# One more GpSimd drain behind an output scatter, in a masked attention layer on one Trainium2 core

## The chip, the cores and the metric

The kernel runs on one core of a Trainium2 chip. Its engines work side by side, each from its own instruction queue: TensorE (PE; its weight loads are shown as PEld), VectorE (DVE), ScalarE (ACT), GpSimd (POOL) and SyncE (SP). Transfers are issued from the queues of SP, ACT and POOL and run on 16 DMA engines. The metric is device time in microseconds for one execution; lower is better. The kernel before takes 637.19 us (median of three runs, 636.75 to 637.22).

## What is computed

One graph attention layer with a norm ahead of it, over 2708 nodes of 1024 features, all in float32:

```python
h = jnp.maximum(_layernorm(x, axis=-1), 0.0)
q = h @ W_q.T + b_q
k = h @ W_k.T + b_k
v = h @ W_v.T + b_v
z = (q @ k.T) / sqrt(1024)
spare_z = z * adj
spare_z = jnp.where(spare_z == 0.0, -10000.0, spare_z)
out = jax.nn.softmax(spare_z, axis=1) @ v
return x + jax.nn.relu(out)
```

The adjacency is sparse: each entry is one with a chance of 0.0014771, about four neighbours for a node.

## The kernel before

The kernel does not form the 2708 x 2708 scores. It folds the two weights of query and key into one matrix `M`, finds the neighbours of each node in `adj`, sorts the nodes by their number of neighbours, and handles 128 sorted nodes at a time (a tile). For a tile it gathers the normed rows of the neighbours one slot at a time, forms the scores and the weighted sum `u` of those rows on VectorE, and multiplies `u` by the value weights on TensorE.

TensorE's work is a list of 20 units (`units`, L1194): ten pairs of tiles for the queries, then ten pairs for the outputs (`o_pairs`, L1192), and one last tile alone. The tiles of the outputs go in the order 6, 5, 4, 3, 2, 0, 20, 7, 17, 13, 18, 12, 19, 11, 15, 10, 14, 1, 16, 9, and tile 8 is the one alone. A pair is multiplied in seven products of blocks (Strassen's scheme in Winograd's form); `multiply` (L1044) issues them, and calls `after(i)` at seven points of each pair, i from 0 to 6. `after` (L1243) interleaves everything else: the attention of later tiles, loads, and the sending of results.

The pair before the last is number `len(units) - 2`, tiles 14 and 1. Its step 2 comes when the second of its products has been copied out.

Results go out like this. ScalarE writes a finished tile `y`; `due` (L1130, L1134) notes at which step it may be sent. `add_due` (L1166) then issues from GpSimd an accumulating gather that adds the rows of `x` in the sorted order to `y` (`add_x`, L1106), and `send` (L1173) issues behind it the scatter of an earlier `y` to its rows of the output (`scatter`, L807). So gathers and scatters alternate in GpSimd's queue, and a scatter belongs to a tile two behind. Every scatter is appended to `outs` (L805). For the last pair and the tile alone, `ends` (L1138) and the code from L1373 gather `x` ahead, and VectorE adds it. The four buffers of the tag "q" hold `y`, so a gather into one waits for the scatter that read it. The tile alone is scattered in two halves (`scatter_half`, L1365).

The order on VectorE is the one written in the code; from L1256 on, the order in GpSimd's queue is made by the tile framework's planner, and `issue_after(ins)` adds a bound, that what it holds is not issued before `ins`.

At the end, `flag` is read by every engine (L1388); it is zero here, and the branch of L1389 skips the general path. When the tile context of L1562 closes, a program end is written: SyncE waits for all outstanding semaphores, every engine drains and the engines meet at a barrier. The program's opening stands at L1555.

Of the kernel before, what the change touches and what calls it, by code (L numbers as in the profile page):

```python
# [65 lines left out]
def tile_preln_masked_attention(  # L66
# [12 lines left out]
    nc = tc.nc  # L79
# [675 lines left out]
    def banks_for(row):  # L755

        return_ = []
        for h in range(NH):
            return_.append(psum.tile([P, NB], FT, tag="acc", name=f"ps{h}"))
            nc.scalar.copy(return_[h], row[:, h * NB:(h + 1) * NB])  # L760
        return return_
# [43 lines left out]
    outs = []  # L805
# [238 lines left out]
    def multiply(n, results, after):  # L1044


        X, Z = banks_of.pop(n)
        ops = ops_of.pop(n)[0]
        Y, p5 = opened_of.pop(n)
        after(0)  # L1050
        after(1)
        products.append(add_block(Y, ops["s2"], T[:, 1]))
        u2 = small("u2")
        nc.scalar.copy(u2, Y)
        after(2)
        add_block(X, ops["a12"], M[:, 1, 0])
        results[0](X)
        after(3)
        products.append(add_block(Z, ops["s4"], M[:, 1, 1]))
        results[2](Z, u2)  # L1060
        after(4)
        products.append(add_block(Y, ops["s3"], T[:, 2]))
        results[1](Y, p5)
        after(5)
        between(n)
        add_block(Y, ops["a22"], T[:, 3])
        results[3](Y)
        after(6)
# [125 lines left out]
    units = [("q",) + p for p in q_pairs] + [("o",) + p for p in o_pairs]  # L1194
# [34 lines left out]
    for n, unit in enumerate(units):  # L1229
# [13 lines left out]
        def after(i):  # L1243
# [81 lines left out]
                single["rows"], = load_rows(("o", alone))  # L1325
            if nxt is None and i == 3:
                single["banks"] = banks_for(bp_sb)
            if n == last_q - 1 and i == 4:

                nc.sync.dma_start(bp_sb, bv.to_broadcast([P, D]))  # L1330
# [235 lines left out]
```

## Time and profile before

| | |
|---|---|
| median of three runs | 637.19 us |
| span of the profiled execution, first to last instruction | 635.2 us |
| PE busy | 624.2 us, 98% |
| DVE busy | 523.9 us, 82% |
| POOL busy | 367.3 us, 58% |
| ACT busy | 285.9 us, 45% |
| granted TensorE clock, mean | 0.996 |

The profiled execution is one of its own. The profile gives its span and no time for what lies before the first instruction and behind the last; the median of the runs is 1.99 us over the span. A row of the page's second part is a strip of 40 slices of the span, each digit the busy share in tenths. In a row of the timeline stand start, duration, engine, line, operation, output and input, and in brackets the idle time before it with what ended it. Names such as POOLq and SPq are an engine's queue (its sequencer): drains, semaphores, branches and DMA issues of SP and ACT stand there, and count as no busy time. A row for one line gives the least, median and largest duration in ns, then the first and last start in us. A row of waits gives the total in us, the number and the longest.

### The profile page before, as it was taken

The numbers are of one execution on the slowest core, as the hardware profiler recorded it, in microseconds if no ns is written. First come the engines' busy times: TensorE is split into PE (matmuls) and PEld (weight loads), VectorE is DVE, ScalarE is ACT, GpSimd is POOL, SyncE is SP. The second block draws the span as 40 slices with busy tenths as digits, with TensorE's granted clock in tenths as the row PEclk, the third lists the DMA queues.
The fourth block names the chain that finished last, engine by engine and source line by source line (L and its number), as shares of the span: only waits on it lengthen the run. The fifth ranks groups of instructions, "written<-read, shape, count | busy, mean of one in ns | idle before, by whom it ended". The sixth has DMA issues, their size and how long they took to land.

```text
span 635.2 us, 6138 instructions
## 1 busy us (share of the span) xinstructions
PE 624.2 (98%) x1627; PEld 316.4 (50%) x1627; DVE 523.9 (82%) x1020; ACT 285.9 (45%) x423; POOL 367.3 (58%) x397
## 2 busy tenths in 40 slices
PE   9999999999999999999999999999999999999993
PEld 5777766444444544444444444444444444444441
DVE  5999888998896755997889999999899999898231
ACT  3538985749667553424341244343343342432200
POOL 2639960885877277564742644586678868622421
PEclk9999999999999999999999999999999999999998
DMA  8999997598796539996599997999999989993851
GB/s 340 407 369 310 342 356 288 203 325 310 261 360 237 182 118 323 342 351 220 188 295 365 307 399 227 322 346 294 386 354 289 336 276 284 278 269 80 242 189 37
DMA packets 62497, 181.16 MB, mean 285 GB/s; under 512 B 10055, under 2 KB 17047, under 8 KB 61688
## 3 DMA queue, kind: packets, MB, share of 16 engines
q0 software_dynamic: 27088, 86.02, 42.6%
q1 hardware_dynamic: 29434, 73.63, 33.2%
q10 hardware_dynamic: 5934, 21.06, 8.5%
q8 instruction: 15, 0.25, 0.1%
q14 instruction: 26, 0.21, 0.1%
HBM read 148.27 MB, written 42.31 MB: 300 GB/s over the span
## 4 chain that ended last, share of the span: by engine, by line
PE 98%; POOL 0%; DVE 0%; POOLq 0%; issue 0%
PE ps L1010 45%; PE psy L1010 32%; PE ps_y L476 6%; PE ps_z L476 4%; PE ps_x L476 4%; PE pt L415 4%; PE ps_y L511 1%; PE ps_h L1222 0%; PE ps_v L594 0%; DVE y_alone L1382 0%; POOL out_dram L1366 0%; POOLq L1388 0%; POOL hsum L121 0%; PE ps_all L680 0%; PE ps_in L678 0%
## 5 line engine op out<-in xcount | busy, mean ns | idle before, releaser
L610 POOL DMA_INDIRECT g<-h_dram,tab x94 | 119.6, 1272 | 62.1 <-ACT u L912 19.1
L1010 PE MATMUL ps<-M,a 128*128 128x512 f32 x320 | 144.0, 593 | 0.0
L1010 PE MATMUL psy<-wlow,s 128*128 128x512 f32 x320 | 143.9, 593 | 0.0
L863 DVE SCALAR_TENSOR_TENSOR junk<-g,pq 128x1024 uint8<-128x1024 f32 x93 | 113.7, 1223 | 12.8 <-DMA g<-h_dram,tab 8.9
L1010 PE MATMUL ps<-M,s 128*128 128x512 f32 x240 | 107.9, 593 | 0.0
L1010 PEld LDWEIGHTS ps<-M,a 128*128 128x128 f32 x320 | 59.9, 190 | 70.7 <-issue 70.0
L1010 PEld LDWEIGHTS psy<-wlow,s 128*128 128x128 f32 x320 | 59.8, 190 | 70.0 <-issue 69.1
L923 DVE SCALAR_TENSOR_TENSOR u<-g,coef,u 128x1024 f32<-128x1024 f32 x69 | 88.4, 1282 | 6.9 <-ACT u L912 5.8
L389 DVE FIND_INDEX8 at<-ones,adj 128x8 uint32<-128x685 f32 (+1 forms) x88 | 74.5, 864 | 0.0
L1010 PEld LDWEIGHTS ps<-M,s 128*128 128x128 f32 x240 | 45.6, 190 | 57.1 <-issue 55.9
L1010 PE MATMUL psy<-wlow,a 128*128 128x512 f32 x160 | 71.9, 593 | 0.0
L368 ACT ACTIVATE sized<-adj 128x2708 uint8<-128x2708 f32 (+1 forms) x22 | 54.3, 2467 | 7.3 <-DMA adj<-in_adj_dram 6.0
L298 POOL TENSOR_TENSOR hsum<-hsum,x 128x256 f32<-128x256 f32 (+1 forms) x56 | 38.6, 726 | 26.2 <-DVE wlow L444 21.6
L1109 POOL DMA_INDIRECT y<-in_x_dram,tab x19 | 32.7, 1723 | 30.5 <-ACT y L1126 15.7
L1010 PEld LDWEIGHTS psy<-wlow,a 128*128 128x128 f32 x160 | 30.5, 190 | 38.2 <-issue 37.5
L1010 PE MATMUL ps<-wlow,s 128*128 128x512 f32 x80 | 36.0, 592 | 0.0
L912 ACT ACTIVATE u<-g,coef 128x1024 f32<-128x1024 f32 x18 | 20.7, 1148 | 29.9 <-DVE coef L911 29.8
L808 POOL DMA_INDIRECT out_dram<-y,tab x21 | 25.3, 1206 | 15.2 <-DVE flag L1357 7.1
L626 POOL DMA_INDIRECT tab_dram<-tab,pos_i x22 | 21.9, 993 | 18.8 <-DVE pos_i L689 13.3
L276 ACT ACTIVATE x<-x,r 128x1024 f32<-128x1024 f32 (+1 forms) x22 | 25.9, 1233 | 7.2 <-POOL r L266 7.2
L944 ACT COPY v<-u 128x1024 f32<-128x1024 f32 x13 | 13.6, 1046 | 32.5 <-DVE u L923 28.2
L476 PE MATMUL ps_y<-wlow 128*128 128x512 f32 x64 | 27.6, 593 | 0.0
(252 smaller groups left out, 851.7 us busy)
## 6 DMA issues: line engine op xcount, KB each, us to landing
adj<-in_adj_dram SPq DMA_DIRECT2D x21, 1354.0 KB, 10.4
x<-in_x_dram SPq DMA_DIRECT2D x21, 512.0 KB, 11.0
h_dram<-x ACTq DMA_DIRECT2D x21, 512.0 KB, 7.3
u_dram<-v ACTq DMA_DIRECT2D x13, 512.0 KB, 6.6
or<-u_dram SPq DMA_DIRECT2D x52, 128.0 KB, 6.4
q_late<-q SPq DMA_DIRECT2D x12, 512.0 KB, 7.1
pq<-q_late POOLq DMA_DIRECT2D x12, 512.0 KB, 8.0
M<-in_wv_dram SPq DMA_DIRECT2D x4, 1024.0 KB, 10.4
```

The source lines that it names most:

```text
L276: nc.scalar.activation(xs[i][:n], xs[i][:n], AF.Relu, bias=r[:n, 4, i:i + 1], scale=r[:n, 3, i:i + 1])
L298: small.append(nc.gpsimd.tensor_add(hsum[:n, cols], hsum[:n, cols], xt[:n, cols]))
L368: nc.scalar.activation(sized[:n], a[:n, :, :PW], AF.Abs, accum_out=total[:n, t:t + 1])
L389: nc.vector.max_index(at[:n, k - first_k, g, :], ones[:n, 0:8], a[:n, g, :])
L415: nc.tensor.transpose(pt[:, c, :], xt[:, k * P:(k + 1) * P], ident)
L476: mm = nc.tensor.matmul(bank, a_tile(o + H * a[0], a[1], i), b(o), start=first and o == 0, stop=(o == H - 1), skip_group_check=True)
L610: return nc.gpsimd.indirect_dma_start(out=dst, out_offset=None, in_=src, in_offset=off, bounds_check=N - 1, oob_is_err=False)
L808: to = nc.gpsimd.indirect_dma_start(out=out, out_offset=bass.IndirectOffsetOnAxis(ap=ptab.bitcast(U32)[:n, t, SLOTS:SLOTS + 1], axis=0), i ...
L863: chained(lambda: nc.vector.scalar_tensor_tensor(junk, g_of[t][s], 1.0, tq[t], op0=ALU.mult, op1=ALU.mult, accum_out=zall[:, t, s:s + 1]))
L923: chained(lambda: nc.vector.scalar_tensor_tensor(u, g_of[t][s], coef[:, s:s + 1], u, op0=ALU.mult, op1=ALU.add))
L1010: mm = nc.tensor.matmul(bank, a[:, c, :], b[:, c, :], start=False, stop=(c == 3), skip_group_check=True)
L1109: return nc.gpsimd.indirect_dma_start(out=y[:n], out_offset=None, in_=x, in_offset=off, compute_op=ALU.add)
```

## The change

Three lines in `after`. When the pair before the last is at step 2, one drain is issued on GpSimd, not before the scatter that was appended last to `outs`. No other line is touched; later lines move down by three.

```diff
@@ -1325,6 +1325,9 @@
                 single["rows"], = load_rows(("o", alone))
             if nxt is None and i == 3:
                 single["banks"] = banks_for(bp_sb)
+            if (n, i) == (len(units) - 2, 2):
+                with tc.issue_after(outs[-1].ins):
+                    nc.gpsimd.drain()
             if n == last_q - 1 and i == 4:
 
                 nc.sync.dma_start(bp_sb, bv.to_broadcast([P, D]))
```

## The prediction

> **What bounds the kernel now.** I read the page first, for the share of each engine and the chain that ended last.
>
> ```profile
> span 635.2 us, 6138 instructions
> PE   9999999999999999999999999999999999999993
> q0 software_dynamic: 27088, 86.02, 42.6%
> PE 98%; POOL 0%; DVE 0%; POOLq 0%; issue 0%
> ```
>
> TensorE sets the pace: the chain is 98% matmul, and no slice but the last shows it idle. A change on GpSimd can matter in two ways only. It makes TensorE wait, or it alters what lies behind the last matmul. So I read the end next: the chain of waits in its last microseconds, then every instruction that stands at line 1562, which is the close of the program (its common barrier).
>
> ```profile
> 615.00 10.42 PE ps L1010 x24
> 625.42 0.02 issue
> 625.45 0.70 DVE y_alone L1382
> 626.15 0.03 issue
> 626.18 0.50 POOLq L1388
> 626.68 0.69 POOL out_dram L1366
> ...
> L1562 SPq EVENT_SEMAPHORE  x14: 17/28/28, 629.7 to 635.2; - x14
> L1562 POOLq EVENT_SEMAPHORE  x4: 17/17/17, 634.4 to 635.1; - x4
> L1562 POOLq DRAIN  x3: 46/109/7122, 627.2 to 634.9; - x3
> L1562 SPq DRAIN  x3: 7/7/13, 630.4 to 634.6; - x3
> L1562 ACTq DRAIN  x2: 8/8/8, 616.5 to 634.6; - x2
> L1562 PEldq DRAIN  x2: 8/8/8, 625.6 to 634.7; - x2
> L1562 DVEq DRAIN  x2: 10/14/17, 629.2 to 634.7; - x2
> ...
> SPq L1562 <- DMA out_dram<-y_alone,half_i: 10.3, 1, 10.3
> SPq L1562 <- PEq L1562: 4.6, 2, 4.1
> ```
>
> The last matmul ends at 625.4, and 9.8 us follow. The chain stops at the last scatter (626.68 + 0.69 = 627.37), since a drain is not counted as work; the rows of line 1562 show what is behind it. They give duration as least/median/most, and the starts of the first and last instruction. ScalarE, TensorE and VectorE come to the barrier at 616.5, 625.6 and 629.2. SyncE first waits for the last scatter to land (its first semaphore row starts at 629.7), goes through the other semaphores and drains at 630.4. GpSimd's first drain starts at 627.2, lasts 7122 ns and so ends at 627.24 + 7.12 = 634.36. Only then do GpSimd's semaphores run, from 634.4. SyncE sits 4.1 us in one wait of this barrier, though the name beside it is that of TensorE's queue, which had arrived at 625.6; GpSimd was the one missing. **So the last 3.9 us before 634.4 belong to GpSimd's drain alone.** SyncE's own arrival is its first drain at 630.42 plus the next about 0.07 later, 630.49, and 634.36 - 630.49 = 3.87.
>
> Then I asked what such a drain costs. The other drains of GpSimd are the two short ones of that row (46 and 109 ns) and one at the opening:
>
> ```profile
> L1555 POOLq DRAIN  x1: 184/184/184, 0.4 to 0.4; - x1
> ```
>
> These three have no transfer of GpSimd between them and the drain or the start before. The long one has all of them: the 27088 packets of the software queue.
>
> **The change, part by part.** It adds one drain on GpSimd and an order (not before the scatter that was issued last); it removes nothing and moves no line. Where it stands:
>
> ```profile
> 571.15 1.57 POOL L1109 DMA_INDIRECT y<-in_x_dram,tab  x1 [9.03 <-ACT y L1133]
> 573.03 1.00 POOL L808 DMA_INDIRECT out_dram<-y,tab  x1 [0.30 <-issue]
> 586.05 1.70 POOL L1109 DMA_INDIRECT y<-in_x_dram,tab  x1 [12.03 <-ACT y L1126]
> 588.06 1.05 POOL L808 DMA_INDIRECT out_dram<-y,tab  x1 [0.31 <-issue]
> 594.34 0.97 POOL L612 DMA_INDIRECT y<-in_x_dram,tab  x1 [5.24 <-DMA out_dram<-y,tab]
> ```
>
> In the pair before the last (tiles 14 and 1), the scatter issued last at step 2 is that of 573.03. GpSimd is then idle from 574.03 to 586.05, waiting 12.03 us for ScalarE's result for tile 14. The drain falls into this hole.
>
> *Cost in the hole.* No row shows a drain in mid-run. From below it is 0.05 us (the 46 ns row). From above it is the whole 7.12 us, and if it first waits for the scatter's landing (median 5.8 us from issue, in the row below, so 578.8), it ends at 585.9. VectorE is busy there 11.45 of 11.80 us, and one scatter's descriptors have taken from 952 to 1884 ns; were the drain stretched by that 1.98, 14.1 us from 574.03 end at 588.1. I take 6.5 us: the last drain runs 634.36 - 627.37 = 6.99 us behind the last scatter, and 25072 of 27088 packets lie before the hole, 93%. It ends near 580.5, under cover of the wait for tile 14.
>
> ```profile
> 574.10:585.90 11.80, 11.80 (x29) 5.18 (x28) 11.45 (x13) 2.69 (x5) 0.00 (x0) 1.00 0.31 83
> L808 POOL DMA_INDIRECT out_dram<-y,tab x21: 952/1041/1884, 415.4 to 615.9; - x21
> out_dram<-y,tab POOLq DMA_INDIRECT x8, 5.8
> ```
>
> *What queues behind it, if the cover is gone.* First the accumulating gather of 586.05, then the scatter of 588.06, then the gather for tile 16 at 594.34, which waits for a scatter to free its buffer. That gather lands in 6.5 us at the median, at 600.8, and its user on VectorE runs at 603.63: 2.8 us to spare. Behind that user, ScalarE refills a bank (604.32 + 0.59 = 604.91), which TensorE reads at 607.85: 2.9 more. TensorE would lose time only from a drain longer than 12.0 + 2.8 + 2.9 = 17.7 us, and none of the bounds reaches that. So this term is 0.
>
> ```profile
> y<-in_x_dram,tab POOLq DMA_INDIRECT x6, 6.5
> 603.63 0.65 DVE L1144 SCALAR_TENSOR_TENSOR y<-ps,y 128x512 f32<-128x512 f32 x1
> 604.32 0.59 ACT L760 COPY ps<-bp_sb 128x512 f32<-128x512 f32 x1 [5.98 <-DVE y L1144]
> 607.85 3.60 PE L1010 MATMUL ps<-M,T_alone 128*128 128x512 f32 x8
> ```
>
> *What it does to the last drain.* Behind the hole GpSimd has 2016 of the 27088 packets left, 7.4%:
>
> ```profile
> q0 software_dynamic: 2016, 7.28, 38.6%
> ```
>
> The unknown is what the 6.99 us are made of. If they grow with what GpSimd has sent since the drain before, 7.4% remain, 0.5 us. If they are the price of any transfer at all, all 6.99 stay. The rows of drains with nothing behind them (46 to 184 ns) show that it isn't a fixed price of a drain. The new last drain, at 7.4% of the packets, is nearer to those than to the 7122 row, so I take 0.5 us; it ends at 627.37 + 0.5 = 627.9. Or it waits for the last landing (629.7) first and then needs 7.4% of the 4.7 us behind that, 0.3: 630.0. Either is before SyncE's 630.49, so **SyncE's arrival is next in line**, and nothing earlier than 3.87 us can be gained.
>
> The Trainium skill, "VectorE: DVE Perf Modes", section "The DRAIN you can't avoid", speaks against all this: drains of the opening and the close are about 12 ns, constant, on all five engines. By it the sum would be nothing. In this trace SyncE, ScalarE, TensorE and VectorE agree with it (7 to 17 ns), and GpSimd's 46 to 7122 ns do not.
>
> *Sum.* Profiled span 635.2 - 3.87 + 0 = 631.3 us. The median of the runs is 637.19, 1.99 more than this span, and I add that unchanged: **633.3 us**, 0.6% faster.
>
> **Rivals.**
>
> 1. *Only part of the drain follows the count.* Say half of the 4.7 us behind the last landing is the price of having any transfer to close: the drain ends at 629.7 + 2.35 = 632.0, the saving is 2.3 us, the time 634.9. For it: the drain outlasts the landing by 4.7 us whatever it does. Against: nothing splits it.
>
> 2. *The last drain stays as it is.* It may pay for closing a queue once per stretch with transfers, be it 13 or 213 of them. Then the new drain costs the same 7 us in the hole, the last one ends at 634.36 again, and the time is 637.2. For: only one drain in the trace has transfers behind it, so nothing shows growth. Against: only that the two short drains cost nothing, which fits this rival as well.
>
> 3. *A drain of a few ns*, nothing added and nothing saved: 637.2 too. The four other engines' rows speak for it, the 7122 row against. The Trainium skill's section "The DRAIN you can't avoid" (page "VectorE: DVE Perf Modes") would give this; the trace does not bear it out for GpSimd.
>
> 4. *Slower: the drain stands late in GpSimd's queue.* The order on GpSimd is the planner's at this point; the edit only bars an earlier place. It decides from the point where the drain falls between the two half scatters of the last tile (the second at 626.41):
>
> ```profile
> 623.77 0.97 POOL L1366 DMA_INDIRECT out_dram<-y_alone,half_i  x1 [6.93 <-DVE y_alone L1379]
> 626.41 0.96 POOL L1366 DMA_INDIRECT out_dram<-y_alone,half_i  x1 [1.67 <-DVE y_alone L1382]
> ```
>
> From 624.74 it runs 7.1 us to 631.9 and holds the last scatter 5.5 us. The landing (3.3 us) comes at 635.2, SyncE's semaphores (0.8) at 636.0, the barrier's 0.8 at 636.8: 1.6 us over, 638.8. For: the hole before the first half is 6.93 us, so any place from there on is exposed. Against: the planner takes work in the order written unless it isn't ready, and a drain needs nothing.
>
> **Chances.** The forecast 0.58; rival 1 0.14; rival 2 0.14; rival 3 0.01; rival 4 0.13. Three runs lie within 0.07%, so a measurement tells about 0.2%, 1.3 us, from no change. The forecast and nearly all of rival 1 are faster than 635.9: faster 0.71, same 0.16 (rivals 2 and 3 and the rest of 1), slower 0.13. The forecast's own range is 632.7 to 634.1: SyncE's arrival bounds it from below, less 0.4 for the spread of the runs, and a last drain that ends 0.8 late from above. For 8 in 10 the range takes in rivals 1 to 3, from 632.6 to 637.6; rival 4 is left out.
>
> **What would show it.** In the new profile, a GpSimd drain of 5 to 9 us starts near 574 and ends before 586; the gather of tile 14 still follows ScalarE's result near 586; the last matmul still ends near 625.4. GpSimd's largest drain at the close falls under 3 us, SyncE's long wait of 4.1 us vanishes, and the span is near 631.3. The forecast is wrong if the closing drain keeps its 7 us (rival 2), if it keeps some 4 to 5 (rival 1), or if the new drain isn't at 574 (rival 4).

## The result, and the profile after

The changed kernel takes 633.37 us (median of four runs, 632.95 to 633.91) against 637.15 us for the kernel before (four runs, 636.75 to 637.22). The ratio is 0.9942, with a 95% interval from 0.9928 to 0.9956. The forecast was 633.3 us, the range 632.6 to 637.6. Measured again beside the experiments, the changed kernel took 633.15 us, ratio 0.9934 (0.9917 to 0.9950).

The page's first line, the new drain's row, and the rows at the close, which now is line 1565:

```profile
span 631.8 us, 6139 instructions
...
L1330 POOLq DRAIN  x1: 11734/11734/11734, 571.5 to 571.5; - x1
...
L1565 SPq EVENT_SEMAPHORE  x14: 17/28/28, 630.1 to 631.7; - x14
L1565 POOLq DRAIN  x3: 46/109/3087, 627.6 to 631.5; - x3
L1565 SPq DRAIN  x3: 7/7/13, 630.9 to 631.2; - x3
L1565 DVEq DRAIN  x2: 10/14/17, 629.5 to 631.2; - x2
```

GpSimd's closing drain fell from 7122 to 3087 ns. It starts at 627.60 and so ends at 630.68, while SyncE's own drains come at 630.87 and 630.94. Before, GpSimd was 3.87 us behind SyncE; now it is there first, by 0.26 us, and SyncE ends the program. The waits of SyncE's queue say the same, where the 4.1 us wait of before has shrunk to 0.5:

```profile
SPq L1565 <- DMA out_dram<-y_alone,half_i: 10.4, 1, 10.4
SPq L1565 <- PEq L1565: 0.7, 2, 0.5
```

Next, GpSimd's timeline around the new drain, and the last lines of the chain:

```profile
573.38 1.00 POOL L808 DMA_INDIRECT out_dram<-y,tab  x1 [0.30 <-issue]
586.42 1.70 POOL L1109 DMA_INDIRECT y<-in_x_dram,tab  x1 [12.03 <-ACT y L1126]
...
626.77 0.96 POOL L1369 DMA_INDIRECT out_dram<-y_alone,half_i  x1 [1.67 <-DVE y_alone L1385]
```

```profile
615.35 10.42 PE ps L1010 x24
625.77 0.02 issue
```

The drain's row begins at 571.5, ahead of the scatter at 573.38, since it is recorded from where the sequencer takes it; it ends at 571.51 + 11.73 = 583.24. The gather of tile 14 still waits 12.03 us for ScalarE, exactly as before, so 3 us of the hole were left over. The last matmul ends at 625.77 (625.42 before). These 0.35 us were there ahead of the drain: the scatter in front of it starts at 573.38, and started at 573.03 before. The whole saving lies behind it: 634.36 - 630.94 = 3.4 us of the profiled span. The medians differ by 3.8.

### The profile page after: what moved, and what is told of

The parts are those of the page before. It is cut to its first block, busy times and chain, and to the rows that moved or that the text cites. A ratio compares the mean times of both kernels' runs of the same rounds, so it can differ in the third digit from the quotient of the medians.

```text
span 631.8 us, 6139 instructions
## 1 busy us (share of the span) xinstructions
PE 624.4 (99%) x1627; PEld 315.7 (50%) x1627; DVE 523.8 (83%) x1020; ACT 286.2 (45%) x423; POOL 366.4 (58%) x397
## 4 chain that ended last, share of the span: by engine, by line
PE 98%; DMA 1%; DVE 0%; POOL 0%; POOLq 0%; issue 0%
PE ps L1010 46%; PE psy L1010 33%; PE ps_y L476 7%; PE ps_x L476 4%; PE ps_z L476 4%; PE pt L415 4%; DMA wlow<-in_wq_dram 1%; PE ps_h L1222 0%; PE ps_v L594 0%; DVE y_alone L1385 0%; POOL out_dram L1369 0%; POOLq L1391 0%; PE ps_in L678 0%; PE ps_all L680 0%; PE ps_b L775 0%
## 5 line engine op out<-in xcount | busy, mean ns | idle before, releaser
L944 ACT COPY v<-u 128x1024 f32<-128x1024 f32 x13 | 13.6, 1046 | 31.8 <-DVE u L923 27.6
L760 ACT COPY ps<-bp_sb 128x512 f32<-128x512 f32 x42 | 24.6, 596 | 7.1 <-DVE y L1144 6.5
```

## Experiments

Two questions were left: what a drain's length is made of, and what the hole's cover is worth. All durations below are of one profiled execution; times are medians of several runs.

**1. Drains by themselves.** A kernel of transfers and drains on GpSimd, in this form (`landed` is a memset of the source, so it waits for all transfers):

```diff
+    for k in range(64):
+        nc.gpsimd.dma_start(room[18 + k], src)
+    landed()
+    nc.gpsimd.drain()
```

> A kernel with nothing but transfers and drains on GpSimd: it copies x to the output and leaves the whole attention layer out. Stretches of transfers of GpSimd are each followed by a memset that waits until all of them have landed, and then a drain, so that the drain's length holds no landing. From before and after: behind the last landing the closing drain took 4.7 us with 213 transfers since the drain before, and 0.7 us with 13, that is 0.4 us + 20 ns a transfer. By the count of transfers: 1 gives 0.44 us, 16 give 0.74, 64 give 1.7, 64 tiny ones (one row of 64 bytes) give 1.7 too, and 16 that are cut into eight times as many pieces give 0.74. By the packets (0.16 ns a packet): 64 tiny ones give 0.45, 16 cut ones about 3. By a price once for any stretch with transfers: all stretches alike, 1 or 64. By the time since the drain before: the shortest stretches least, whatever they send. 16 that are not waited for: the landing and 0.74. Nothing sent, or SyncE's transfer alone outstanding: 0.05 to 0.2 us.

Rows of its drains, in order (1, 16, 64, 64 tiny, 16 cut, 16 not waited for, none, and a second one with none, behind SyncE's transfer in the code), then the row of SyncE's transfer:

```profile
L43 POOLq DRAIN  x1: 483/483/483, 27.6 to 27.6; - x1
L47 POOLq DRAIN  x1: 1702/1702/1702, 45.5 to 45.5; - x1
L51 POOLq DRAIN  x1: 5617/5617/5617, 83.3 to 83.3; - x1
L55 POOLq DRAIN  x1: 5627/5627/5627, 121.8 to 121.8; - x1
L59 POOLq DRAIN  x1: 1697/1697/1697, 138.7 to 138.7; - x1
L62 POOLq DRAIN  x1: 4462/4462/4462, 147.2 to 147.2; - x1
L64 POOLq DRAIN  x1: 399/399/399, 152.0 to 152.0; - x1
L66 POOLq DRAIN  x1: 47/47/47, 152.4 to 152.4; - x1
...
L65 SPq DMA_DIRECT2D out_dram<-in_x_dram x1: 582/582/582, 0.7 to 0.7; - x1
DMA to landing us min/median/max: 38.4/38.4/38.4
```

The memset that the drain has to let end is in these, and 399 ns is what it gives with nothing sent. Above that, 1 transfer costs 84 ns, 16 cost 1303 and 64 cost 5218: **81.5 ns a transfer**. Transfers of one row of 64 bytes cost as much as those of 128 KB (5627 against 5617 ns, with 2048 packets against 3072). The count decides, at four times the slope that the expectation took from the two closing drains. The price once for a stretch (rival 2) is ruled out. The cut transfers made no more packets in the trace than the whole ones, so they tell nothing. The 16 that were not waited for cost less behind their landing: it came at 150.95, and the drain ended 0.69 us later, at 151.64.

The last of these drains did not meet SyncE's transfer, which had been issued at 0.7 us and landed at 39.1. But the first row answers the question: the drain of 27.6 ended at 28.1, with that transfer still under way, so it isn't waited for.

**2. Longer stretches, indirect gathers, VectorE busy.** The same with 32, 96, 128 and 200 transfers, 128 indirect gathers, and 64 transfers with VectorE working on two SBUF inputs through the whole drain.

> Again transfers and drains of GpSimd alone, with x copied to the output and the attention layer left out. In the first such kernel a drain behind landed transfers took 0.40 us with none, and 81.5 ns more for each transfer (16 and 64 of them, whatever their size). By that line without an end: 32 transfers give 3.0 us, 96 give 8.2, 128 give 10.8, 200 give 16.7. But the kernel before had 213 and its drain took 7.0 us from the last scatter's end, which is about 80 transfers at that price. If what is left to be closed has a ceiling near 80: 32 give 3.0, and 96, 128 and 200 give all about 7, with the transfers behind the 80th longer to issue. If the price is less in a long stretch (a wait and a smaller price each): 96, 128 and 200 rise on, but by less than 81.5 ns each. 128 indirect gathers: as 128 plain ones. 64 with VectorE busy on two inputs in SBUF: 5.6 as without it; if VectorE's work holds GpSimd up, 6.5 to 11.

```profile
L47 POOLq DRAIN  x1: 3021/3021/3021, 51.3 to 51.3; - x1
L49 POOLq DRAIN  x1: 8241/8241/8241, 107.5 to 107.5; - x1
L51 POOLq DRAIN  x1: 2187/2187/2187, 186.6 to 186.6; - x1
L53 POOLq DRAIN  x1: 8067/8067/8067, 297.9 to 297.9; - x1
L59 POOLq DRAIN  x1: 1990/1990/1990, 475.6 to 475.6; - x1
L64 POOLq DRAIN  x1: 5617/5617/5617, 513.9 to 513.9; - x1
```

Up to 96 the line holds (0.4 + 96 x 0.0815 = 8.2). Then all three guesses fail: 128 transfers cost 2.2 us, which is 22 of them, and 200 cost 8.1, which is 94. In both, 106 had been closed on the way. The 128 indirect gathers cost 2.0 us, near the 128 plain ones. VectorE's work doesn't stretch the drain here: 5617 ns with it and without.

**3. Where the line breaks.** 104, 112, 116 and 160 transfers, then 32, 64 and 96 indirect gathers.

> Transfers and drains of GpSimd alone, x copied to the output, no attention layer. The kernel before this one gave 0.4 us + 81.5 ns a transfer up to 96 transfers, but 2.2 us behind 128 (22 transfers' worth) and 8.1 behind 200 (94): 106 had been closed on the way, and the 114th came after a pause. If GpSimd closes what it has each time its store is full, which is at the 114th: 104 give 8.9 us, 112 give 9.5, 116 give 1.2 (10 transfers' worth), 160 give 4.8 (54). If it closes some all the time behind the hundredth: 104 to 116 all near 8.5, falling slowly. For indirect gathers, 32 give 3.0, 64 give 5.6, 96 give 8.2 if the price is one for a transfer of any kind; 128 gave 2.0.

Its drains in that order, and a piece of GpSimd's timeline in the stretch of 116:

```profile
L54 POOLq DRAIN  x1: 8905/8905/8905, 89.5 to 89.5; - x1
L56 POOLq DRAIN  x1: 9547/9547/9547, 160.1 to 160.1; - x1
L58 POOLq DRAIN  x1: 1207/1207/1207, 234.3 to 234.3; - x1
L60 POOLq DRAIN  x1: 4784/4784/4784, 323.6 to 323.6; - x1
L62 POOLq DRAIN  x1: 2807/2807/2807, 374.7 to 374.7; - x1
L64 POOLq DRAIN  x1: 5416/5416/5416, 464.9 to 464.9; - x1
L66 POOLq DRAIN  x1: 8029/8029/8029, 599.4 to 599.4; - x1
```

```profile
170.10 59.95 POOL L27 DMA_DIRECT2D room<-src  x113 [9.72 <-issue]
230.87 1.60 POOL L27 DMA_DIRECT2D room<-src  x3 [0.82 <-issue]
```

It is a saw: the debt grows by 81.5 ns a transfer up to 9.5 us behind 112, the 114th comes after a pause of 0.8 us, and 106 are gone. Indirect gathers rise by nearly the same, 81.7 ns (8029 - 5416 = 2613 for 32), though each makes 144 packets against 48:

```profile
q0 software_dynamic: 13824, 50.34, 98.5%
...
dst<-in_x_dram,idx POOLq DMA_INDIRECT x96, 8.5
```

```profile
q0 software_dynamic: 5376, 14.69, 68.7%
...
room<-src POOLq DMA_DIRECT2D x112, 128.0 KB, 2.2
```

**4. The drain in a later hole**, between the scatters at 616 and at 624 us, in place of the one at 574.

```diff
     nc.vector.scalar_tensor_tensor(y[:, hi], p1, 0.0, y[:, hi], op0=ALU.max, op1=ALU.add)
+    with tc.issue_after(outs[-2].ins):
+        nc.gpsimd.drain()
     scatter_half(1, hi)
```

> The drain stands in a later hole of GpSimd, between the scatter of 616.2 us and the first half scatter of 624.1, which only 2 transfers follow. By the count: it ends near 624.1, no work is late by more than 0.4 us, the closing drain is 0.45 us behind the landing (with 13 transfers it was 0.7), and the time is that of the changed kernel, 633.4 +- 0.4, since SyncE comes last at the barrier. If GpSimd's drain still set the end in the changed kernel, 0.25 us less: 633.1. If the drain doesn't fit its hole and holds up the end: 634 to 635.

```profile
L1381 POOLq DRAIN  x1: 8327/8327/8327, 615.8 to 615.8; - x1
...
L1564 POOLq DRAIN  x3: 46/103/2187, 627.6 to 631.1; - x3
L1564 SPq DRAIN  x3: 7/7/13, 630.5 to 630.8; - x3
```

633.40 us, ratio 0.9938 (0.9921 to 0.9954): the changed kernel's time. With 2 transfers left, GpSimd is done at 629.8, still earlier than with 13, and nothing is gained by it: **SyncE's arrival is the floor.** The drain itself ends at 624.10, and the first half scatter goes 1.0 us later without harm (GpSimd is idle for 7.94 us ahead of it, 6.93 before).

**5. The drain between the two half scatters**, where the last scatter stands right behind it: the place and price of the prediction's rival 4.

```diff
     scatter_half(1, hi)
+    with tc.issue_after(outs[-1].ins):
+        nc.gpsimd.drain()
     add_block(X, uT[:, 4:8, :], M[:, 1, 0])
```

> The drain stands between the two half scatters of the last tile, where nothing covers it. By the count (0.4 us + 20 ns a transfer behind the landing): first half landed near 626.5 us, 212 transfers 4.7 us, drain ends 631.2, last scatter lands at 634.5, SyncE comes 0.8 later, 0.8 for the barrier: span 636.2, time 638.2, 0.16% slower than before; the closing drain is 0.5 us behind the landing. If any stretch with transfers costs the whole 7 us: span 640.6, time 642.6. If a drain in mid-run cost nothing and took nothing off the closing one: 637.2.

```profile
L1382 POOLq DRAIN  x1: 7614/7614/7614, 623.5 to 623.5; - x1
...
L1564 POOLq DRAIN  x3: 46/109/2429, 632.7 to 636.4; - x3
...
631.80 0.96 POOL L1366 DMA_INDIRECT out_dram<-y_alone,half_i  x1 [7.15 <-issue]
```

638.66 us, ratio 1.0024 (1.0014 to 1.0034). The last scatter is held from 626.4 to 631.80. The closing drain is short again, so what was saved there is paid here, and 1.5 us more. Rival 4 had named 638.8 us.

**6. The drain four pairs earlier**, where GpSimd has no hole: `(len(units) - 6, 2)` in place of `(len(units) - 2, 2)`.

> The drain stands four pairs earlier (tiles 17 and 13, near 470 us), where GpSimd has no hole and some 68 transfers follow. By the count: closing drain 0.4 + 68 x 0.02 = 1.8 us behind the landing, ends 0.9 us behind SyncE: time 634.3 if the halt of GpSimd (landing of the last transfer, 8 us, and 0.4 + 145 x 0.02 = 3.3 us) is hidden, and up to 11 us more if TensorE has to wait for the gathers behind it. If the closing drain pays only once for a first stretch: closing drain 0.7 us, 633.4 if hidden.

```profile
L1330 POOLq DRAIN  x1: 15633/15633/15633, 468.1 to 468.1; - x1
...
L1565 POOLq DRAIN  x3: 46/109/5513, 631.9 to 638.0; - x3
L1565 SPq DRAIN  x3: 7/7/13, 634.9 to 637.7; - x3
...
DVE junk L863 <- DMA wlow<-h_dram,tab: 9.4, 2, 7.5
```

639.57 us, ratio 1.0029 (1.0016 to 1.0041), with a wide spread (636.97 to 640.45). Two effects add up. GpSimd stands still until 483.8 and VectorE later waits 7.5 us for a gather; the last matmul ends at 630.1, 4.3 us later than in the changed kernel. And the 65 transfers that follow have built up a closing drain of 5.5 us, which ends at 637.4, 2.5 us behind SyncE. The 1.8 us of the expectation was meant behind the last landing. That came at 634.10, so 3.3 us lay behind it: the slope taken from the two closing drains was too low. At 81.5 ns, 65 transfers would give 5.3; the row's 5.5 is near that, but 2.2 of it are spent before the landing. (The planner also swapped a few GpSimd transfers here.)

**7. The hole filled without a drain.** 16, then 22 memsets of a dead tile stand in the hole, and the gather of tile 14 is ordered behind them.

```diff
+            if (n, i) == (len(units) - 2, 2):
+                for _ in range(16):
+                    with tc.issue_after(outs[-1].ins):
+                        stay.append(nc.gpsimd.memset(hsum, 0.0))
```

> No drain; 16 memsets of a dead tile (about 15 us) hold GpSimd from 574 us on, so that the gather of tile 14 comes near 589.5 in place of 586.05. The prediction worked out 17.7 us from 574.0 to the first loss of TensorE. By that: no loss, 637.2, the closing drain as before (7 us). If GpSimd's queue is tighter than that: up to 3.4 us more, 640.6.

```profile
574.13 16.10 POOL L1333 MEMSET hsum<- 128x1024 f32 x16
590.39 1.57 POOL L1109 DMA_INDIRECT y<-in_x_dram,tab  x1 [0.15 <-issue]
...
L1568 POOLq DRAIN  x3: 46/109/6902, 627.0 to 634.5; - x3
```

636.69 us, ratio 0.9992 (0.9982 to 1.0001): not slower, although the gather of tile 14 is 4.3 us late, and not faster than noise. The closing drain keeps its 6.9 us. So holding GpSimd in this hole saves nothing; the drain does.

> The same with 22 memsets (about 21 us, to 595), 3.3 us over the 17.7: TensorE waits and the time is near 640.5. If GpSimd's queue has more room than worked out: 637.2. If tighter: up to 646. (The planner also puts one accumulating gather ahead of two scatters here.)

```profile
574.56 22.15 POOL L1333 MEMSET hsum<- 128x1024 f32 x22
596.87 1.57 POOL L1109 DMA_INDIRECT y<-in_x_dram,tab  x1 [0.16 <-issue]
...
608.38 3.60 PE L1010 MATMUL ps<-M,T_alone 128*128 128x512 f32 x8
612.03 0.59 ACT L760 COPY ps<-bp_sb 128x512 f32<-128x512 f32 x1 [13.16 <-DVE y L1144]
...
PE psy L1010 <- DVE p L1150: 3.1, 1, 3.1
```

641.51 us, ratio 1.0077 (1.0060 to 1.0093). Here the gather is 10.8 us late, 0.5 of it already at the scatter ahead of the memsets (it ends at 574.56, and at 574.03 before). TensorE waits 3.1, so some 7.2 us were to spare behind 586.05, where 5.7 had been worked out.

**8. The changed kernel once more.**

> The changed kernel once more, for the spread of the landings: 633.4 +- 0.5 us; the mid drain ends 9 us behind its scatter, the closing drain 3 us behind the last scatter, and GpSimd comes to the barrier before SyncE by 0.1 to 0.5 us.

Its new drain ended 8.8 us behind its scatter, and the closing drain (2762 ns from 627.2) at 630.0, before SyncE's 630.25: as expected, at 633.15 us.

## Why the prediction was right

- *What ended the program.* GpSimd's drain, 3.87 us behind everyone else: right. It went, and the others came to the barrier in the order of before.
- *SyncE's arrival is next in line.* Right, and shown twice: in the changed kernel SyncE ends the program, and with only 2 transfers left (experiment 4) the time stays where it is. It came 0.45 us later than in the old trace, as the matmuls ended 0.35 later in this execution; hence 3.4 us of span in place of 3.87.
- *The new drain costs nothing in its hole.* Right. Its length was under-sized: 6.5 us forecast, 8.9 us from the scatter's end (574.38 to 583.24), inside the upper bound of 585.9. The feared stretch by VectorE's work did not show in experiment 2, where the drain took 5617 ns with VectorE busy and with VectorE idle.
- *17.7 us of cover.* Right in kind: none lost at 16.1 us, 3.1 us at 22.2. The path behind the gather was read wrongly. It was to run over ScalarE's refill of a bank to the matmul of 607.85; with 22 memsets that matmul runs at 608.38, before the refill at 612.03, so it does not need it. TensorE waited for VectorE's addition at line 1150, which stands behind the gather's user, and there was some 1.5 us more room.
- *The last drain grows with what was sent since the drain before.* Right, on less evidence than it needed, since one long drain can't show a slope. The share by packets was the wrong measure: behind landed transfers their number decides, at 81.5 ns each up to 112 of them. By that price the 4.7 us behind the last landing stand for about 58 of the 213, and the 7 us from the last scatter's end for 86 at most. For 13 transfers 0.5 us was forecast behind the last scatter; it was 630.68 - 627.73 = 2.95, and 0.6 behind the landing (630.1), where 0.3 had been put. SyncE's floor hid the difference, with 0.26 us to spare (0.27 in experiment 8), where 2.6 and 0.5 us had been worked out. That the time came out so near has some luck in it.
- *Rivals.* Rival 1 (a part stays whatever is sent) leaves 0.1 us behind the landing with 1 or 2 transfers, far from its 2.35. Rival 2 falls with experiment 1, rival 3 with any of the rows. Rival 4 was the right price for a place that the planner did not choose. The Trainium skill's 12 ns ("VectorE: DVE Perf Modes", "The DRAIN you can't avoid") is stated for the runtime's drains of preamble and postamble, while those here stand at lines of the kernel. It is near the four other engines' 7 to 17 ns after the change as before it, and as far from GpSimd's 11734 and 3087 ns as from the 7122.

Two things stay open. In this kernel the break of the saw could not be placed: by the count alone 107 of 213 transfers should be left at the end, 8.7 us by the price, and the drain is shorter. Scatters and accumulating gathers were not tried apart. Nor was it settled how much a drain closes while it still waits for the last landing. Behind it lay 0.1 us with 1 or 2 transfers, 0.6 with 13 (1.06 by the price; the expectations have 0.7), 3.3 with 65 (5.3 by the price), 5.4 with the 200 of the new drain, and between 4.6 and 4.7 with 211 to 213, although that landing came from 1.7 to 2.5 us behind the end of its scatter.

## What to carry to other kernels

When the chain of waits stops before the span ends, read the rows of the program's close: the engine that reaches the barrier last owns that time. If it is GpSimd with a long drain behind many transfers, one drain in a hole late in the program pays that debt early. Put it where the hole holds the landing and 81.5 ns for each transfer to be closed (the longest drain behind landed transfers took 9.5 us), and where few transfers follow. In a stretch without a hole, or right ahead of the last transfer, it cost more here than it saved: 2.4 us more than the kernel before in experiment 6, and 1.5 us more in experiment 5.

## What the runs showed that was not expected

A drain on GpSimd pays for the transfers sent since the drain before: 81.5 ns for each (8029 against 5416 ns for 96 and 64 indirect gathers, 5617 against 399 for 64 plain ones and none), whatever its size and packets, also when all have landed. But in the kernels of transfers alone the 114th behind a drain came after a pause of 0.8 us, and 106 no longer had to be paid for, where a drain of 112 took 9.5 us: 4 transfers more, and the drain took 1.2. By that, a kernel's closing drain could change by microseconds when a few transfers are added or taken away far from the end; in the attention kernel this was not tried.
